# Edges of a graph sorted by half tiles of targets: two scaled one-hots side by side on TensorE, sums of eight fixed pairs kept in PSUM, empty slots masked

## The chip, the cores and the metric

The kernel runs on one core of a Trainium2 chip. The core has TensorE (PE), VectorE (DVE), ScalarE (ACT), GpSimd (POOL) and SyncE (SP), each with its own queue of instructions, and 16 DMA engines that all queues share. The metric is the device time of one execution in microseconds (us).

## What is computed

A layer over 3125 nodes of 512 features and 50000 edges. A node's features are a scalar part of 128 and three vector parts of 128. The layer is a graph convolution plus linear attention, followed by a mixture of eight experts of which each node takes two. The change is in the graph convolution, whose edge part is this:

```python
w = ssp(edge_attr @ W_f1) @ W_f2 * (ssp(s0 @ W_s1) @ W_s2)
w1, w2, w3, w4 = jnp.split(w, 4, axis=-1)
x0e, x1e = split_irreps(x[edge_src])
sh0, sh1 = (edge_sh[:, 0], edge_sh[:, 1:4])
out0 = w1 * x0e * sh0[:, None] + w4 * (jnp.einsum('eum,em->eu', x1e, sh1) / jnp.sqrt(3.0))
out1 = w2[:, :, None] * x0e[:, :, None] * sh1[:, None, :] + w3[:, :, None] * x1e * sh0[:, None, None]
edge_feat = merge_irreps(out0, out1)
out = jax.ops.segment_sum(edge_feat, edge_dst, num_segments=old_x.shape[0])
```

Each edge has four numbers sh. Each of the eight products of weights and source features is multiplied with one of them, and the results are summed over the edges of a target node. The part s0 needs, for each edge, the products of the vector parts at its two ends.

## The kernel before

**Tiles of edges.** Edges come in any order. The kernel sorts them by tiles of 125 targets (TG, 25 tiles), so that the sum over edges becomes a product of a one-hot matrix (edge to target in the tile) with the features. Edges are taken 128 at a time; two such blocks are a pair (PR = 2), two pairs a quad (G = 4 blocks). A tile gets as many pairs as its edges need; 204 pairs are always run (NPR_MOST), and 16 more stand in a branch for data that needs them.

**The sort and the node work (lines 129 to 654).** DVE counts the edges of each tile (line 201, one instruction for each of 25 tiles), and `places` (lines 230 to 252) ranks the edges of a chunk of 28 blocks: a comparison of tiles (235), a running sum (239), a product (243), a reduction (244), and some index arithmetic. `records` builds a record of 48 numbers for each edge (sh, source, target, place in the tile, hidden activations) and writes it to memory in line. Then POOL scatters the records to their sorted places, 391 indirect DMAs of 128 records (417). `place` lets POOL go on only as far as PE has come in the node work beside it. All slots of the sorted list are zeroed first (166, 10 DMAs from POOL), since a tile's last pair has empty slots.

**The edge loop (lines 709 to 978).** Order on PE, ACT, DVE and POOL is written out by hand in `run_pairs`. One step s handles, of different pairs: `fetch` (four indirect gathers on POOL, two of 1664 and two of 3584 bytes a row; nine pairs ahead), `products` (DVE, both ends of an edge), `turn` and `hidden` (PE: transposes and small products, for a quad), `softplus` (ACT), `weigh` (PE makes two factors of the weights, ACT scales the first and copies it, DVE multiplies), `dots` and `dots2` (ACT and DVE: the sum over sh of the vector parts), `feats` (DVE, and six ACT scalings by sh: 1024 features for each edge), `which` (DVE: the one-hot, 128 wide), `gather_up` and `keep_sums`:

```python
for k in range(PR):
    for m in range(2):
        nc.tensor.matmul(
            R.ps, R.one[:, k, :], R.ft[:, k, m * D : (m + 1) * D],
            start=(k == 0 and m == 0), stop=(k == 1 and m == 1),
        )
```

Four matrix products of 512 columns give a pair's sums in PSUM; each appears in the profile as two instructions (passes)[...]. DVE then adds them to the tile's row of acc. `line_up` copies the experts' weights into another layout, memory to memory, 32 DMAs of 1 MB on POOL's queue, one in every sixth step.

**The experts (from line 983).** Tile by tile, own rows are loaded (1020), the sums of acc are transformed and added, stored (1031), normed and stored again (1051). Then the gates, index arithmetic and 53 expert tiles.

Of the kernel before, what the change touches and what calls it, by code (L numbers as in the profile page):

```python
# [16 lines left out]
P = 128  # L17
EDGES = 50000
TG = 125
D = 512  # L20
# [11 lines left out]
NPR_MOST = 204  # L32
# [13 lines left out]
def gnn_mix_moe_kernel(ctx: ExitStack, tc: tile.TileContext, a: dict, out: bass.AP):  # L46
# [13 lines left out]
    NPR = (EDGES - NG) // (PR * P) + NG  # L60
    whole, rest_e = divmod(EDGES, P)
    TE = whole + (rest_e > 0)
    NQ = (NPR * PR + G - 1) // G
# [29 lines left out]
    pair_tile = const.tile([P, NPR], I32, name="pair_tile")  # L93
# [4 lines left out]
    lined = dram.tile([T // CT, P, CT, REC], F32, name="lined")  # L98
    recs = dram.tile([NQ * G * P, REC], F32, name="recs")

# [19 lines left out]
    tok = counted(const, "tok", [[TG, NT]], [P, NT], channel=1)  # L120
# [8 lines left out]
    with ExitStack() as c1:  # L129
        srt = c1.enter_context(tc.tile_pool(name="srt", bufs=1))  # L130
        ints = c1.enter_context(tc.tile_pool(name="ints1", bufs=1))
        pair_no = counted(srt, "pair_no", [[1, NPR]], [P, NPR])
# [21 lines left out]
        for r in range(4):  # L154
# [5 lines left out]

        zw = NQ * G * REC // 10
        zero = tmp.tile([P, zw], F32, name="zero")
        nc.vector.memset(zero, 0.0)
        flat = recs.rearrange("s f -> (s f)")
        cleared = [
            nc.gpsimd.dma_start(
                flat[k * P * zw : (k + 1) * P * zw].rearrange("(p f) -> p f", p=P), zero
            )
            for k in range(10)
# [16 lines left out]
        in_tile_i = tmp.tile([P, T], I32, name="in_tile_i")  # L186
        nc.vector.tensor_scalar(in_tile_i, to_i, 4195.0, None, op0=ALU.mult)
        nc.vector.tensor_single_scalar(in_tile_i, in_tile_i, 19, op=ALU.arith_shift_right)
        in_tile = tmp.tile([P, T], F32, name="in_tile")
        nc.vector.tensor_copy(in_tile, in_tile_i)  # L190
        to_f = tmp.tile([P, T], F32, name="to_f")
        nc.vector.tensor_copy(to_f, to_i)
        local = tmp.tile([P, T], F32, name="local")
        nc.vector.scalar_tensor_tensor(local, in_tile, -float(TG), to_f, op0=ALU.mult, op1=ALU.add)

        NC = T // CT
        hot = tmp.tile([P, NT, CT + 1], F32, name="hot")
        sums = tmp.tile([P, NT], F32, name="sums")
        here = tmp.tile([P, T], F32, name="here")
        for b in range(NT):  # L200
            nc.vector.tensor_scalar(
                here, in_tile, float(b), 0.0, op0=ALU.is_equal, op1=ALU.add, accum_out=sums[:, b : b + 1]
            )
        ps_c = psum.tile([P, NT], F32, name="ps_c", tag="mm")
# [224 lines left out]
        for c in range(1, NC):  # L429
            records(c)  # L430
            for t in range((c - 1) * NT // (NC - 1), c * NT // (NC - 1)):
                place(8 * t + 42)
                place(8 * t + 50, layer_norm(t))
# [997 lines left out]
```

## Time and profile before

| what | value |
|---|---|
| median of 3 runs | 2956.8 us (2954.85 to 2974.9) |
| the profiled execution | 2957.7 us, its span 2955.8 us |
| PE busy | 2533.0 us, 86% |
| DVE busy | 1785.0 us, 60% |
| POOL busy | 1719.6 us, 58% |
| ACT busy | 1393.6 us, 47% |
| first scatter of records | 79.23 us |
| first gather of the edge loop | 721.87 us |
| first aggregation (line 902) | 774.41 us |
| last addition to acc (line 911) | ends 2022.8 us |

The page has the busy time of each engine, the same in 40 slices of the span, and groups of instructions by line. In a group's row come line, engine, operation, output and inputs, shapes and count; then its busy time and the mean ns of one; then the time for which its engine stood idle before it, and what ended that. A row of the timeline has start, duration, engine, line, operation, and in brackets the idle time before it. PEld is the loading of PE's stationary operand.

### The profile page before, as it was taken

What the parts mean: (1) busy time and instruction counts of PE and PEld (TensorE: products, weight loads), DVE (VectorE), ACT (ScalarE), POOL (GpSimd) and SP (SyncE); (2) the same over time, 40 slices, a digit from 0 to 9 for tenths busy, and PEclk for the clock granted to TensorE, in tenths of its full rate; (3) what the DMA queues carried; (4) which work ended last, traced back from release to release, by engine and by line L of the source; (5) the groups of instructions that cost most, each with busy time, mean ns of one, the idle gap of its engine ahead of it and who ended that gap; (6) DMA issues with size and microseconds to landing.
All of it is one profiled execution on the core that took longest, in us unless ns stands there. A gap on an engine that the chain in (4) does not pass through costs nothing. (4 is left out here: it accounts for less than half of the span.)

```text
span 2955.8 us, 44464 instructions
## 1 busy us (share of the span) xinstructions
PE 2533.0 (86%) x14742; PEld 1593.7 (54%) x14742; DVE 1785.0 (60%) x3666; ACT 1393.6 (47%) x3960; POOL 1719.6 (58%) x1723
## 2 busy tenths in 40 slices
PE   2466594885699999999999999997599999999997
PEld 2344242553344444444444444445488888888886
DVE  4755450223699999999999999998422222222221
ACT  1334241110588888877888888885211111111111
POOL 0766657664766666666666666641355555555552
PEclk9767796897799999999999999999799999999998
DMA  6435202554788888787888888855722623956361
GB/s 259 148 126 175 85 21 66 168 174 137 245 256 255 256 255 254 256 248 247 254 259 262 261 263 262 253 177 187 279 66 72 239 69 119 329 202 244 112 223 51
DMA packets 189190, 577.23 MB, mean 195 GB/s; under 512 B 54177, under 2 KB 78662, under 8 KB 176920
## 3 DMA queue, kind: packets, MB, share of 16 engines
q0 software_dynamic: 132912, 485.72, 51.1%
q1 hardware_dynamic: 49704, 82.29, 8.2%
q10 hardware_dynamic: 6336, 6.28, 0.7%
q8 instruction: 121, 1.98, 0.3%
q14 instruction: 117, 0.96, 0.1%
HBM read 624.55 MB, written 119.50 MB: 252 GB/s over the span
## 5 line engine op out<-in xcount | busy, mean ns | idle before, releaser
L902 PE MATMUL ps_s<-ft,one 128*128 128x512 f32 x1632 | 745.7, 600 | 19.4 <-issue 14.2
L730 POOL DMA_INDIRECT gd<-rows_d,rec x408 | 434.4, 1065 | 269.0 <-issue 87.2
L417 POOL DMA_INDIRECT recs<-again,at_i x391 | 400.8, 1025 | 231.6 <-issue 110.5
L902 PEld LDWEIGHTS ps_s<-ft,one 128*128 128x128 f32 x1632 | 294.1, 190 | 396.0 <-issue 318.7
L734 POOL DMA_INDIRECT gx<-rows_s,rec x408 | 400.9, 983 | 144.8 <-issue 102.4
L885 ACT ACTIVATE ft<-ft,rec 128x128 f32<-128x128 f32 x1224 | 380.2, 389 | 201.9 <-DVE ft L878 143.0
L1306 ACT ACTIVATE h<-ps_f,bias 128x128 f32<-128x128 f32 x318 | 110.7, 367 | 671.5 <-PE ps_f L1293 622.1
L1293 PE MATMUL ps_f<-h,we 128*128 128x128 f32 x3392 | 406.8, 278 | 16.7 <-ACT h L1306 15.1
L1293 PEld LDWEIGHTS ps_f<-h,we 128*128 128x128 f32 x3392 | 388.8, 192 | 30.7 <-ACT h L1306 25.0
L1308 DVE TENSOR_SCALAR h<-ps_f,bias 128x128 f32<-128x128 f32 x318 | 108.2, 350 | 481.6 <-PE ps_f L1293 456.9
L1220 POOL DMA_INDIRECT we<-w_rows,w_at x212 | 214.3, 1011 | 266.6 <-PE ps_y L1324 102.0
L830 DVE TENSOR_TENSOR wt<-wt,wb 128x1024 f32<-128x1024 f32 x204 | 247.6, 1214 | 29.9 <-PE ps_h L775 21.9
L840 ACT ACTIVATE dot<-gx,rec 128x128 f32<-128x128 f32 x816 | 261.4, 398 | 0.0
L819 PE MATMUL wa<-w_f,hT 32*128 32x512 f32 x816 | 240.2, 642 | 3.7 <-issue 2.6
L823 PE MATMUL wb<-w_s,hT 32*128 32x512 f32 x816 | 241.7, 644 | 0.0
L1293 PEld LDWEIGHTS ps_f<-xt,we 128*128 128x128 f32 x1696 | 200.1, 194 | 26.0 <-issue 24.9
L746 DVE TENSOR_TENSOR prod<-gd,gx 128x768 f32<-128x768 f32 x204 | 194.0, 951 | 31.0 <-DMA gx<-rows_s,rec 31.0
L1293 PE MATMUL ps_f<-xt,we 128*128 128x128 f32 x1696 | 200.5, 277 | 0.7 <-ACT xt L1241 0.7
L754 PEld LDWEIGHTS ps_ip<-ident,prod 128*128 128x128 f32 x1224 | 136.3, 144 | 118.7 <-issue 118.7
L889 DVE TENSOR_TENSOR ft<-gx,wt 128x768 f32<-128x768 f32 x204 | 197.6, 969 | 0.0
L1324 PE MATMUL ps_y<-we,h 128*128 128x512 f32 x424 | 196.1, 605 | 0.2
L754 PE MATMUL ps_ip<-ident,prod 128*128 128x128 f32 x1224 | 161.3, 283 | 40.7 <-issue 40.7
(306 smaller groups left out, 3599.2 us busy)
## 6 DMA issues: line engine op xcount, KB each, us to landing
w_rows<-in_Wh POOLq DMA_DIRECT2D x24, 1024.0 KB
rows_s<-r SPq DMA_DIRECT2D x24, 448.0 KB
recs<-zero POOLq DMA_DIRECT2D x10, 1056.0 KB
rec<-recs SPq DMA_DIRECT2D x102, 96.0 KB
lined<-rec SPq DMA_DIRECT2D x14, 672.0 KB
again<-lined POOLq DMA_DIRECT2D x14, 672.0 KB
w_rows<-in_Wo POOLq DMA_DIRECT2D x8, 1024.0 KB
gd<-rows_d,rec POOLq DMA_INDIRECT x408
```

The costliest lines, as they stand in the source:

```text
L417: put = nc.gpsimd.indirect_dma_start(out=recs[:, :], out_offset=bass.IndirectOffsetOnAxis(ap=at_i[:m, t : t + 1], axis=0), in_=again[c][:m ...
L730: nc.gpsimd.indirect_dma_start(out=Q.gd[:, (i + 2) % G, :], out_offset=None, in_=rows_d[:, :], in_offset=bass.IndirectOffsetOnAxis(ap=reci ...
L734: Q.last = nc.gpsimd.indirect_dma_start(out=Q.gx[:, i, :], out_offset=None, in_=rows_s[:, :], in_offset=bass.IndirectOffsetOnAxis(ap=reci[ ...
L754: nc.tensor.matmul(ps[:, i, :], Q.prod[:, i, b * P : (b + 1) * P], ident, is_transpose=True, start=(b == 0), stop=(b == 2),)
L819: nc.tensor.matmul(wa[:, k, :], Q.hT[r, 0, :], w_f2[r, :], start=True, stop=True)
L823: nc.tensor.matmul(wb[:, k, :], Q.hT[r, 1, :], w_s2[r, :], start=True, stop=True)
L830: nc.vector.tensor_mul(R.wt, R.wt, wb)
L840: nc.scalar.activation(R.dot[:, c - 1, k, :], x[:, i, c * MUL : (c + 1) * MUL], AF.Copy, scale=Q.rec[:, i, c : c + 1])
L885: nc.scalar.activation(R.ft[:, k, D + c * MUL : D + (c + 1) * MUL], R.ft[:, k, 2 * D :], AF.Copy, scale=Q.rec[:, i, c : c + 1],)
L902: nc.tensor.matmul(R.ps, R.one[:, k, :], R.ft[:, k, m * D : (m + 1) * D], start=(k == 0 and m == 0), stop=(k == 1 and m == 1),)
L1220: nc.gpsimd.indirect_dma_start(out=dst, out_offset=None, in_=src, in_offset=bass.IndirectOffsetOnAxis(ap=at[:, j : j + 1], axis=0), bounds ...
L1293: nc.tensor.matmul(pss[f], ws[l][:, k, f * P : (f + 1) * P], h[:, k, :], start=(k == 0), stop=(k == 3))
```

## The change

It does six things.

- Edges are sorted by half tiles: the first 63 and the last 62 targets of a tile's 125. The first block of each pair holds edges of the first half, the second block those of the second. A tile always has eight pairs (PER), so room for 1024 edges a half; what is over goes to 12 overflow pairs at the end (NOV_MOST), and to a loop behind a branch if that isn't enough. 200 + 12 pairs are always run.
- A slot that holds no edge isn't zeroed in memory any more (only each tile's last quad and the overflow pairs are); its record is masked on DVE when it is loaded (`clear`).
- The one-hot is 64 wide, made once for a quad, and ACT makes four copies of it, scaled by the four sh (`scaled`). The features are then no longer scaled: `dots` and `dots2` go, with six scalings on ACT and a multiplication on DVE, and all six products of vector parts come from two DVE multiplications.
- The aggregation has four products a block, one of 512 and three of 256 columns; the two blocks of a pair use the columns 0 to 63 and 64 to 127 of the array.
- The sums of a tile's eight pairs stay in PSUM, and ACT copies them to acc once; only overflow pairs are added on DVE.
- The copies of the experts' weights go to ACT's queue and are written beside the sort and the node work. In the experts' part a tile has 128 rows, so loads and stores come in half tiles, and index arithmetic maps rows to nodes.

```diff
-        in_tile_i = tmp.tile([P, T], I32, name="in_tile_i")
-        nc.vector.tensor_scalar(in_tile_i, to_i, 4195.0, None, op0=ALU.mult)
+        in_half_i = tmp.tile([P, T], I32, name="in_half_i")
+        nc.vector.tensor_scalar(in_half_i, to_i, 4194.0, 1500.0, op0=ALU.mult, op1=ALU.add)
...
-        for b in range(NT):
+        for b in range(NU):
             nc.vector.tensor_scalar(
-                here, in_tile, float(b), 0.0, op0=ALU.is_equal, op1=ALU.add, accum_out=sums[:, b : b + 1]
+                here, in_half, float(b), 0.0, op0=ALU.is_equal, op1=ALU.add, accum_out=sums[:, b : b + 1]
...
             nc.vector.tensor_tensor(
-                hot[:, :, 1:], in_tile[:, c * CT : (c + 1) * CT].unsqueeze(1).to_broadcast([P, NT, CT]),
-                lane[:, :NT].unsqueeze(2).to_broadcast([P, NT, CT]), op=ALU.is_equal,
+                hot[:, :, 1:], in_half[:, ts].unsqueeze(1).to_broadcast([P, NU, CT]),
+                lane[:, :NU].unsqueeze(2).to_broadcast([P, NU, CT]), op=ALU.is_equal,
             )
...
+        def line_up(behind):
+            if not mats:
+                return
+            e, l = mats.pop(0)
+            src = a["Wh"][e, l] if l < NL else a["Wo"][e]
+            with tc.issue_after(behind.ins):
+                nc.scalar.dma_start(
+                    w_rows[l][e * P : (e + 1) * P, :].rearrange("p (k f) -> p k f", k=4),
+                    src.rearrange("(k p) f -> p k f", p=P),
+                )
...
-                place(8 * t + 50, layer_norm(t))
+                normed = layer_norm(t)
+                place(8 * t + 50, normed)
+                line_up(normed)
...
                 place(275 + 5 * (2 * c + g), last)
+                line_up(last)
...
+        def clear(Q, real):
+            reci = Q.rec.bitcast(I32)[:, :, :USED]
+            nc.vector.tensor_tensor(
+                reci, reci, real.rearrange("p s k -> p (s k)").unsqueeze(2).to_broadcast([P, G, USED]),
+                op=ALU.bitwise_and,
+            )
...
+        def which(Q):
+            Q.one = work.tile([P, G, HT], F32, name="one")
+            nc.vector.tensor_tensor(
+                Q.one, lane[:, :HT].unsqueeze(1).to_broadcast([P, G, HT]),
+                Q.rec[:, :, 6:7].to_broadcast([P, G, HT]), op=ALU.is_equal,
+            )
...
+        def scaled(R):
+            R.ones = work.tile([P, PR, 4, HT], F32, name="ones", bufs=3)
+            for k, i in enumerate(R.tiles):
+                for c in range(4):
+                    nc.scalar.activation(
+                        R.ones[:, k, c, :], R.Q.one[:, i, :], AF.Copy, scale=R.Q.rec[:, i, c : c + 1]
+                    )
...
             R.wt = work.tile([P, PR, D], F32, name="wt")
-            for k, i in enumerate(tiles):
-                nc.scalar.activation(
-                    R.wt[:, k, : 2 * MUL], wa[:, k, : 2 * MUL], AF.Copy, scale=Q.rec[:, i, 0:1]
-                )
-            nc.scalar.copy(R.wt[:, :, 2 * MUL :], wa[:, :, 2 * MUL :])
+            nc.scalar.copy(R.wt, wa)
             nc.vector.tensor_mul(R.wt, R.wt, wb)
...
             nc.vector.tensor_mul(
-                ends,
-                R.wt.rearrange("p k (b c u) -> p k b c u", b=2, c=2)[:, :, :, 0, :],
-                x[:, :, :MUL].unsqueeze(2).to_broadcast([P, PR, 2, MUL]),
-            )
...
+                ends, w[:, :, :, 0, :], x[:, :, :MUL].unsqueeze(2).to_broadcast([P, PR, 2, MUL]),
+            )
+            for k in range(PR):
+                nc.vector.tensor_mul(
+                    R.ft[:, k, MUL : 7 * MUL].rearrange("p (b c u) -> p b c u", b=2, c=3),
+                    w[:, k, :, 1, :].unsqueeze(2).to_broadcast([P, 2, 3, MUL]),
+                    x[:, k, MUL:].rearrange("p (c u) -> p c u", c=3).unsqueeze(1).to_broadcast([P, 2, 3, MUL]),
+                )
+
+        def gather_up(R, ps, first, last):
+            for m in range(4):
+                for k in range(PR):
+                    rows = slice(k * HT, (k + 1) * HT)
...
+                    nc.tensor.matmul(
+                        to, R.ones[:, k, m, :], what, start=(first and m == 0), stop=(last and m == 3),
+                        tile_position=(0, k * HT),
                     )
...
+            def kept(at):
...
+                if at >= NFIX:
+                    keep_sums(tile_of(pair_tile[0:1, at - NFIX : at - NFIX + 1]), R.ps)
+                elif at % PER == PER - 1:
+                    nc.scalar.copy(acc[:, at // PER, :], R.ps)
...
+            for s in range(-LEAD - 5, n_pairs + 1):
+                for Q in due(s + LEAD + 5):
+                    q = quads.index(Q)
+                    loaded = load(Q, recs[q * G * P : (q + 1) * G * P, :])
...
+                for Q in due(s + LEAD + 1):
+                    q = quads.index(Q)
+                    clear(Q, real_slot[:, PR * q : PR * (q + 1), :])
+                for R in pair(s + LEAD):
+                    fetch(R.Q, R.j)
+                for Q in due(s + 2):
+                    softplus2(Q)
+                for Q in due(s + 3):
+                    which(Q)
+                for k in range(2):
+                    for Q in due(s + 7 - k):
+                        products(Q, k)
+                for R in pair(s + 1):
+                    weigh(R)
+                kept(s - 1)
...
-                    nc.gpsimd.dma_start(out[rows, :], base[:n, t, :])
+                    for k in range(2):
+                        i0 = t * TG + k * (HT - 1)
+                        m = HT - 1 - k
+                        nc.gpsimd.dma_start(out[i0 : i0 + m, :], base[k * HT : k * HT + m, t, :])
```

## The prediction

> **What bounds the kernel now.** I read first the busy slices of the page, then a table of busy time by stretch. It gives four stages: sorting and node work (0 to 717 us), filling the edge pipeline (717 to 774), the edge loop (774 to 2023), and the gated experts. In the table each engine has its busy time and, in brackets, its instructions; then come the clock granted to PE, the share of the DMA engines and GB/s.
>
> ```profile
> core 0: us, PE busy (x) PEld busy (x) DVE busy (x) ACT busy (x) POOL busy (x), PEclk, DMA share, GB/s
> 79.00:360.00 281.00, 164.83 (x586) 108.29 (x586) 158.20 (x500) 105.68 (x217) 203.06 (x193) 0.76 0.43 139
> 774.00:1960.00 1186.00, 1159.83 (x6568) 540.56 (x6564) 1141.88 (x2025) 968.45 (x2990) 814.30 (x805) 1.00 0.81 256
> ```
>
> In the edge loop PE and DVE are both full (98% and 96%), ACT has 82%, POOL looks free at 69%. The aggregation of line 902 ran 1536 times between 780 and 1960 us, eight instructions a pair: 192 pairs, 6.13 us each. The timeline shows one pair on DVE; the first column is the start, so differences of starts are what an instruction really costs:
>
> ```profile
> 1970.53 0.68 DVE L911 TENSOR_TENSOR acc<-acc,ps_s 128x512 f32 x1
> 1971.13 1.22 DVE L830 TENSOR_TENSOR wt<-wt,wb 128x1024 f32<-128x1024 f32 x1
> 1972.38 0.69 DVE L878 TENSOR_TENSOR ft<-wt,gx 128x512 f32<-128x512 f32 x1
> 1972.99 0.95 DVE L889 TENSOR_TENSOR ft<-gx,wt 128x768 f32<-128x768 f32 x1
> 1973.86 0.42 DVE L894 TENSOR_TENSOR ft<-wt,dot 128x256 f32<-128x256 f32 x1
> 1974.19 0.41 DVE L860 TENSOR_TENSOR one<-lane,rec 128x256 f32<-128x256 f32 x1
> 1974.53 0.42 DVE L848 TENSOR_TENSOR dot<-dot 128x256 f32<-128x256 f32 x1
> 1974.98 0.62 DVE L850 SCALAR_TENSOR_TENSOR dot<-gx,rec,dot 128x128 f32<-128x128 f32 x2
> 1975.51 0.95 DVE L746 TENSOR_TENSOR prod<-gd,gx 128x768 f32<-128x768 f32 x1
> ```
>
> No gap stands between them: 5.85 us, and 6.05 in every other pair, which has line 801 as well. So **DVE sets 5.95 us** of the 6.13.
>
> POOL is not as free as it looks. The groups of the loop, then the timeline of the filling, where POOL waits for nobody:
>
> ```profile
> L730 POOL DMA_INDIRECT gd<-rows_d,rec x349 | 371.4, 1064 | 213.4 <-issue 73.2 <-DVE one L860 46.3 <-PE ps_h L775 39.8
> L734 POOL DMA_INDIRECT gx<-rows_s,rec x348 | 341.1, 980 | 123.0 <-issue 87.2 <-ACT ft L885 32.8 <-ACT wt L829 1.8
> ...
> 733.21 0.94 POOL L734 DMA_INDIRECT gx<-rows_s,rec  x1 [0.30 <-issue]
> 734.46 0.95 POOL L730 DMA_INDIRECT gd<-rows_d,rec  x1 [0.30 <-issue]
> 735.55 0.96 DVE L746 TENSOR_TENSOR prod<-gd,gx 128x768 f32<-128x768 f32 x1 [3.86 <-DMA gx<-rows_s,rec]
> 735.72 1.61 POOL L734 DMA_INDIRECT gx<-rows_s,rec  x1 [0.30 <-issue]
> ```
>
> A gather takes 0.95 us and 0.30 stand before the next, so the four of a pair need at least 5.0 us. The one at 735.72 began while DVE multiplied two SBUF tiles, and took 0.66 more: it got going when DVE was done. With only that product beside it POOL needed 5.5 us a pair here (products at 735.55, 741.11, 746.59). In the loop the stretch averages 0.07 us a gather, so POOL could do 5.3.
>
> **What the Trainium skill says.** "SBUF — State Buffer", section "Who interferes with whom": a DVE tensor_tensor with both inputs in SBUF contends with a GpSimd instruction that reads SBUF, and the second to start waits for the first to end. The trace agrees (the 0.66 us); multiplications with one input in PSUM (line 830) stretched no gather. "TensorEngine Tiling (Array Packing)", section "Tiling Modes": tiles in different columns load and multiply in parallel, but a change of mode drains the array. The trace agrees on the first, at 32 columns:
>
> ```profile
> 1308.56 0.43 PE L770 MATMUL ps_h<-ident,rec 128*32 128x128 f32 x8
> 1308.80 0.40 PE L775 MATMUL ps_h<-ident,gd 128*32 128x128 f32 x8
> 1309.02 0.40 PE L780 MATMUL ps_h<-ip,w_s1c 128*32 128x128 f32 x8
> ```
>
> These 24 passes of 128 columns end after 0.86 us. A pass of 512 columns costs 0.43 us in line 902 (0.19 of loading and 0.24 of idle), so one of 128 costs 0.107, and 24 in a row 2.57. No run shows 64 columns. "Trainium Kernel Development and Optimization", section "Key Constraints": DMAs from the SP, ACT and POOL queues run on the same 16 engines.
>
> **The change, part by part.** Its sum is made against the profiled execution, 2957.7 us (span 2955.8), 0.9 above the median of 2956.8.
>
> DVE, per pair. Gone: the sum over acc 0.60, line 894 0.33, lines 848 and 850 0.98, half of the one-hot 0.17 (256 wide once in two pairs, not in each). New: a second multiplication of 768 elements, 0.87, and the mask of 160 elements in each quad, between the 0.20 of 128 and the 0.33 of 256, halved to 0.12. 5.95 - 2.08 + 0.99 = **4.86 us**.
>
> PE, per pair. The aggregation took 3.60 to 3.70 us for 8 passes of 512 columns; now 4 of 512 and 12 of 256, or 5120 columns for 4096. One after the other that is 4.56 us; two at a time 2.28, and one pass of offset makes 2.7. A quad took 11.35 us (aggregations at 1300.33 and 1311.68), so 5.7 a pair; less 1.0, plus some 0.2 for changes of mode: **4.9 us**.
>
> ACT, per pair. It was 968.45 / 1186 of 6.13, or 5.0. Gone: ten scalings at 0.31 (1.86 for six), and 0.5 as three copies of 0.83 + 0.57 become one of some 0.9. New: eight scalings half as wide, 0.27 each by the slope of line 829 against line 826. About 3.6 us; it hides.
>
> POOL, per pair. Four gathers as before, 5.0, and the stretches. DVE now has three multiplications of 0.87, one of 0.61 and half of mask and one-hot that hold the port. If gathers start at any time in them, the mean wait is the sum of half squares, (3 x 0.82^2 + 0.56^2 + 0.06) / 2 / 5.5 = 0.22, with each hold cut by the 0.13 us by which the stretches stay under the remainder: 5.9 us a pair. The loop's own 0.07 gives 5.3, the filling's case 5.5. I take **5.55**, so POOL becomes the bound. Behind it DVE's products wait for rows, which land 3.8 us after the fourth gather (737.33 to 741.11). The DMA engines were at 0.79 in 740 to 760 us with POOL unhindered, so they do not bind.
>
> The loop then has 212 pairs, not 204 (200 fixed and 12 for overflow; with this data 10 overflow pairs are needed, so the late branch stays untaken, as the branch of before did at 203). 212 x 5.55 = 1177, 4 for the landing, nine pairs without gathers at 4.9 = 44: 1225 us. Before it was 721.9 to 2022.8, 1301. Gain: **76 us**.
>
> The sorting. Counting 50 half tiles, not 25, adds 25 x 0.65 us on DVE before the first edge is placed at 79 us, and the first chunk's ranks 4.5: +20. Zeroing falls from 10.8 MB to 3 MB, which may free the 11 us that DVE waited for sh at 45 us: -5. Then 13 chunks of ranks with DVE steps twice as wide. POOL scatters here at 1.27 us an edge block; of 198 scatters 18 met the scan of line 239 and stretched by 0.56 each, 10 us. Holds twice as long cost four times that: +30, and +10 for the two compares. POOL idled 34 us at 360 to 394 for PE, which takes most of it in: +10 remain. The 32 weight copies (33.5 MB) leave POOL's queue in the loop and go to ACT's queue here. At the loop's 256 GB/s they are 131 us of DMA time on top of 0.43 x 281 = 121: 90% of this stretch, which it may just hold: +13. Issuing them takes ACT up to 1.4 us each (W_kT at 7.02), hidden by its 62% of idle time, unless they stand ahead of its first activation. Together **+38**; bounds -20 and +120, since the trace does not show such copies beside the sort.
>
> The rest. Clearing acc (10.7 us) ran beside the wait for the records: 0. The expert stage reads and writes two half tiles where it had one: POOL 2 x 0.53 us in a period of 1.31, just hidden; four small DVE steps on the gather indices, 0.8 us; two stores of normed rows become one. **+2**. SP's more loads go ahead of need.
>
> 2957.7 - 76 + 38 + 2 = **2922 us**; as a median, 2921.
>
> **The rivals.**
> First, the forecast: POOL binds at 5.3 to 5.9 us, 2849 (with +20 of sorting) to 3010 (with +60). Chance 0.55.
> Second, the slower side: the first stage pays. The line that is to hold the copies back names a PE instruction, while they are ACT's, and copies that wait for nothing could stand at the head of ACT's queue. There 131 us of traffic share the engines with the first loads of edges, and scatters start at some 180, not 79 us. +100 against the 76 gives about 3005; it decides from a growth of 106 us in the first stage. For it: DMA was at 0.74 in the first 50 us and DVE waited 24.6 and 11.1 us for sh. Against: the queues take turns. Chance 0.22.
> Third, the halves do not run side by side: PE at 5.7 + 0.9 + 0.2 = 6.8 us, 212 x 6.8 = 1442 and 52 of filling, +193 and +40: 3190. The 0.86 us speak against. Chance 0.06.
> Fourth, gathers fall between DVE's holds and the sort stays hidden: 5.05 us, 1119, -182 and +10: 2788. Chance 0.17.
>
> **The numbers.** A difference under 1% (29.6 us) can't be told from none here. Faster: 0.33 of the first and all of the fourth, 0.50. Same: 0.16 of the first and 0.08 of the second, 0.24. Slower: the rest, 0.26. The range of 2800 to 3040 leaves out most of the third and a part of the fourth and of the second; the first alone has 2850 to 3010.
>
> **What would show it.** PE in the loop well under 90% with POOL's gaps at 0.30; the new aggregation at 2.3 to 2.9 us a pair; gathers of 1.05 to 1.15 us mean; DVE waiting at line 746 for rows; first scatter at 90 to 105 us; first gather at 740 to 780. Wrong would be: scatters starting past 150 us, an aggregation over 4 us, or a period over 6 us a pair.

## The result, and the profile after

The changed kernel took 3145.3 us (median of 4 runs, 3138.9 to 3157.3), the kernel before 2955.8 us: a ratio of 1.065, 95% interval 1.058 to 1.071. It is slower, by 190 us; 2921 us were forecast. The profiled execution has a span of 3137.2 us, 181.4 more than the 2955.8 of the kernel before. By stage:

| stage | before | after | difference | forecast |
|---|---|---|---|---|
| start to the first gather | 721.9 | 742.7 | +20.8 | +38 |
| first gather to the last sum | 1300.9 | 1470.8 | +169.9 | -76 |
| experts | 933.0 | 923.7 | -9.3 | +2 |

So the whole loss is in the edge loop. The measurements of this study fell on two kinds of occasions, **short** ones, on which the kernel before took 2770 to 2784 us (but for single runs of 2980 and 7487 us, which are left out), and **long** ones like that of the result, on which it took 2942 to 3036 us, so a kernel is compared only with runs of the kernel before on the same occasion.

The table of busy time for the edge loop after the change:

```profile
core 0: us, PE busy (x) PEld busy (x) DVE busy (x) ACT busy (x) POOL busy (x), PEclk, DMA share, GB/s
797.00:2100.00 1303.00, 1112.00 (x8057) 523.70 (x8049) 937.78 (x1249) 719.59 (x2223) 845.52 (x770) 0.88 0.69 207
```

No engine is full: PE 85%, DVE 72%, POOL 65%. PE's clock, which was 1.00, is 0.88, and the DMA engines moved 207 GB/s where they moved 256. The groups of the loop say who waits:

```profile
L829 POOL DMA_INDIRECT gx<-rows_s,rec x424 | 483.7, 1141 | 262.1 <-DVE ft L949 138.5 <-issue 105.7 <-DVE prod L840 10.9
L825 POOL DMA_INDIRECT gd<-rows_d,rec x424 | 445.7, 1051 | 266.5 <-issue 108.1 <-PE ps_h L866 98.9 <-DVE rec L813 29.2
L931 DVE TENSOR_TENSOR wt<-wt,wb 128x1024 f32<-128x1024 f32 x212 | 258.4, 1219 | 382.4 <-ACT wt L930 236.9 <-remote 95.5 <-ACT ones L913 17.1
L840 DVE TENSOR_TENSOR prod<-gd,gx 128x768 f32<-128x768 f32 x212 | 202.3, 954 | 33.9 <-DMA gx<-rows_s,rec 21.5 <-remote 7.9 <-issue 4.5
```

POOL waits for DVE and PE to release gx and gd; DVE waits for ACT's copy of wa, and ACT for PE. A pair takes 6.70 us on the mean (differences of starts of line 931), but the median is 5.90: half of the pairs take 4.9 to 6, and about one in four 7.9 to 10.9. The timeline of PE in such a pair; "issue" stands where the engine waited for nothing that the profile shows:

```profile
895.66 2.37 PE L969 MATMUL ps_s<-ft,ones 128*64 128x512 f32 x16
...
900.83 0.41 PE L861 MATMUL ps_h<-ident,rec 128*32 128x128 f32 x4 [1.08 <-DVE rec L813]
902.03 0.38 PE L861 MATMUL ps_h<-ident,rec 128*32 128x128 f32 x2 [0.79 <-issue]
902.75 0.27 PE L861 MATMUL ps_h<-ident,rec 128*32 128x128 f32 x1 [0.34 <-issue]
903.46 0.37 PE L861 MATMUL ps_h<-ident,rec 128*32 128x128 f32 x1 [0.43 <-issue]
903.49 0.41 PE L866 MATMUL ps_h<-ident,gd 128*32 128x128 f32 x1
904.20 0.37 PE L866 MATMUL ps_h<-ident,gd 128*32 128x128 f32 x1 [0.30 <-issue]
904.90 0.63 PE L866 MATMUL ps_h<-ident,gd 128*32 128x128 f32 x2 [0.33 <-issue]
906.32 0.46 PE L866 MATMUL ps_h<-ident,gd 128*32 128x128 f32 x2 [0.78 <-issue]
...
907.34 3.73 PE L969 MATMUL ps_s<-ft,ones 128*64 128x512 f32 x16
```

The aggregation at 895.66 takes 2.37 us, within the 2.3 to 2.9 forecast. But from 900.8 to 906.3 PE's small products come at 902.03, 902.75, 903.46, 904.20, 904.90: one step each 0.71 us, though the profile shows nothing that they wait for. The same 16 passes took 0.64 us in the kernel before (1308.56 to 1309.20 in the prediction). The aggregation after them takes 3.73 us, since the clock has fallen. Windows of 3.41 us, the step of the clock's records, show which came first:

```profile
896.60:900.01 3.41, 3.08 (x22) 1.00 (x18) 3.32 (x4) 1.07 (x5) 2.50 (x4) 1.00 0.87 283
900.01:903.42 3.41, 1.06 (x7) 0.47 (x8) 1.64 (x4) 0.64 (x2) 2.80 (x3) 0.98 0.74 222
903.42:906.84 3.42, 1.97 (x15) 1.00 (x16) 0.00 (x0) 2.22 (x9) 1.23 (x2) 0.50 0.85 249
906.84:910.25 3.41, 3.41 (x18) 1.36 (x14) 2.69 (x3) 3.05 (x10) 0.94 (x1) 0.52 0.50 165
```

First PE's instructions thin out (7 products in the second window, at 0.98 of the clock; 0.8 us of its idle time is the wait for DVE's rec); the clock is halved from the next window on. POOL gathers all the while, and its own timeline ends with the stretch:

```profile
902.76 0.95 POOL L825 DMA_INDIRECT gd<-rows_d,rec  x1 [0.30 <-issue]
904.01 0.94 POOL L829 DMA_INDIRECT gx<-rows_s,rec  x1 [0.30 <-issue]
907.26 0.94 POOL L825 DMA_INDIRECT gd<-rows_d,rec  x1 [2.30 <-PE ps_h L866]
912.97 0.95 POOL L829 DMA_INDIRECT gx<-rows_s,rec  x1 [4.77 <-DVE prod L840]
```

POOL's last gather of a series ends at 904.95, and by 906.3 PE runs again. This mostly repeats every 27.4 us, four pairs: 15 or 16 gathers with 0.30 us between them, PE slow from about the twelfth on, everything behind PE late, POOL out of buffers, and PE free again. Counted over the loop from the starts of PE's products and weight loads together: of 144 gaps of 0.69 to 0.73 us, 143 lie in a series of gathers or less than 1 us after it, and each of the 40 series of 14 or more gathers has some. Such series, with the 1 us, cover 82% of the time from 800 to 2150 us, so this count points to POOL but proves little by itself. Below, "slow gaps" are these, counted from 60 us after the first gather to 30 us before the last sum (146 here); "half clock" is the time at half clock in the same stretch (324 us here; 7 us and 14 slow gaps in the kernel before). With products alone there are fewer: the expectation of g2_pace3 says 97.

### The profile page after: what moved, and what is told of

It is laid out like the page before. It is cut to its first block, busy times and chain, and to the rows that moved or that the text cites. A ratio compares the mean times of both kernels' runs of the same rounds, so it can differ in the third digit from the quotient of the medians.

```text
span 3137.2 us, 46186 instructions
## 1 busy us (share of the span) xinstructions
PE 2525.6 (81%) x16716; PEld 1592.3 (51%) x16716; DVE 1684.5 (54%) x3084; ACT 1162.2 (37%) x3261; POOL 1822.3 (58%) x1741
## 5 line engine op out<-in xcount | busy, mean ns | idle before, releaser
L829 POOL DMA_INDIRECT gx<-rows_s,rec x424 | 483.7, 1141 | 262.1 <-DVE ft L949 138.5
L969 PE MATMUL ps_s<-ft,ones 128*64 128x256 f32 (+1 forms) x3392 | 588.2, 481 | 17.8 <-issue 15.2
L825 POOL DMA_INDIRECT gd<-rows_d,rec x424 | 445.7, 1051 | 266.5 <-issue 108.1
L459 POOL DMA_INDIRECT recs<-again,at_i x391 | 425.8, 1089 | 236.0 <-issue 111.6
L913 ACT ACTIVATE ones<-one,rec 128x64 f32<-128x64 f32 x1696 | 428.1, 339 | 0.0
L969 PEld LDWEIGHTS ps_s<-ft,ones 128*64 128x64 f32 x3392 | 254.8, 149 | 301.5 <-issue 238.0
L949 DVE TENSOR_TENSOR ft<-wt,gx 128x768 f32<-128x768 f32 x424 | 386.0, 952 | 0.0
L930 ACT COPY wt<-wa 128x1024 f32<-128x1024 f32 x212 | 214.3, 1011 | 424.6 <-PE wb L928 207.0
L928 PE MATMUL wb<-w_s,hT 32*128 32x512 f32 x848 | 270.8, 655 | 11.2 <-issue 8.3
L924 PE MATMUL wa<-w_f,hT 32*128 32x512 f32 x848 | 252.9, 650 | 7.5 <-issue 5.7
L840 DVE TENSOR_TENSOR prod<-gd,gx 128x768 f32<-128x768 f32 x212 | 202.3, 954 | 33.9 <-DMA gx<-rows_s,rec 21.5
```

What stands on the lines that cost most here:

```text
L459: put = nc.gpsimd.indirect_dma_start(out=recs[:, :], out_offset=bass.IndirectOffsetOnAxis(ap=at_i[:m, t : t + 1], axis=0), in_=again[c][:m ...
L825: nc.gpsimd.indirect_dma_start(out=Q.gd[:, (i + 2) % G, :], out_offset=None, in_=rows_d[:, :], in_offset=bass.IndirectOffsetOnAxis(ap=reci ...
L829: nc.gpsimd.indirect_dma_start(out=Q.gx[:, i, :], out_offset=None, in_=rows_s[:, :], in_offset=bass.IndirectOffsetOnAxis(ap=reci[:, i, 4:5 ...
L913: nc.scalar.activation(R.ones[:, k, c, :], R.Q.one[:, i, :], AF.Copy, scale=R.Q.rec[:, i, c : c + 1])
L924: nc.tensor.matmul(wa[:, k, :], Q.hT[r, 0, :], w_f2[r, :], start=True, stop=True)
L928: nc.tensor.matmul(wb[:, k, :], Q.hT[r, 1, :], w_s2[r, :], start=True, stop=True)
```

## The experiments

Three theories of the half clock stood first: IDLE, LOAD and STALL, as the expectations say. Diffs are against the changed kernel.

**e1_zero**: features of zero.

```diff
+        nc.vector.tensor_single_scalar(w_f2, w_f2, 0.0, op=ALU.mult)
```

> The changed kernel with w_f2 multiplied by zero once before the edge loop, so that wa, wt and the features ft that the aggregation streams are all zero; every instruction stays (the messages are left out of the result). Three theories of the 324 us at half clock in the edge loop. IDLE (PE is no longer the full engine, has windows of little work, and loses its clock for it): nothing changes, 3145 us within 30, half clock for 280 to 370 us of the loop. LOAD (two column halves at once draw too much, and the clock is taken for that): zeros draw less, half clock under 80 us, time 2880 to 2950. STALL (something else holds PE's instructions back every 27 us and the clock only follows): as IDLE.

**e2_serial**: the halves one after the other.

```diff
-            for m in range(4):
-                for k in range(PR):
+            for k in range(PR):
+                for m in range(4):
```

> The changed kernel with the two loops of gather_up exchanged: all passes of one half, then all of the other, so that halves no longer run side by side. Same result. The aggregation goes from 2.37 to some 4.4 us a pair and PE is full at 6.8 to 7.1 us a pair. IDLE: a full PE keeps its clock, half clock under 60 us of the loop, 212 x 6.9 = 1463 us of loop and 3110 to 3190 us in all, the same as the changed kernel although 2 us of PE work a pair came on top. LOAD: the clock stays too, same time. STALL: half clock stays over 200 us, time over 3300 us.

**e3_warm**: wa made twice.

```diff
                 nc.tensor.matmul(wa[:, k, :], Q.hT[r, 0, :], w_f2[r, :], start=True, stop=True)
+            for k, i in enumerate(R.tiles):
+                r = slice(i * HID, (i + 1) * HID)
+                nc.tensor.matmul(wa[:, k, :], Q.hT[r, 0, :], w_f2[r, :], start=True, stop=True)
```

> The changed kernel with the products for wa (line 924) made twice, the second time over the first: 4 more passes of 512 columns on PE in each pair, some 0.6 us, same result. IDLE: PE has fewer windows with little work, half clock falls from 324 to under 150 us of the loop, and the time falls, to 2960 to 3080 us, though work was added. LOAD and STALL: half clock stays at 300 us or more, time 3200 to 3280 us.

**e4_light**: half of the aggregation.

```diff
-            for m in range(4):
+            for m in (0, 3):
```

> The changed kernel with half of the aggregation left out (the sums over the first two vector components, m = 1 and 2): 1.1 us less PE work a pair, everything else as it was. IDLE: more windows with little work, half clock at 324 us or more of the loop, and the time hardly falls: 3050 to 3150 us. LOAD: less is drawn, half clock under 150 us, time 2850 to 2930 us. STALL: half clock at 250 to 330 us, time 3000 to 3100 us.

All four missed on the time, since this was a short occasion: 2769.1, 2821.5, 2766.3 and 2766.3 us, where the kernel before took 2777.5. That called for both kernels as they are.

> The changed kernel itself, once more, beside the four edits of the first experiments, which took 2766 to 2821 us where the kernel before took 2777.5 and not 2955.8. SUPPLY (in the first profiles PE's instructions came for stretches one each 0.71 us although nothing held them, in the kernel before as well, and the changed kernel, which hands PE 84 instructions a pair in place of 68 and in bursts, pays more for it; the edits did nothing of weight): 2755 to 2785 us here, half clock in the edge loop under 150 us, hardly a gap of 0.69 to 0.73 us between PE's instructions. LOAD or IDLE (the edits did it, each in its own way): 3100 us or more here, with 0.71 us gaps and 280 us or more at half clock.

> The kernel before itself, for its profile at 2777 us. SUPPLY: its first stage is shorter by 60 to 100 us (first gather at 620 to 660 us, not 722), its edge loop by 50 to 70 (5.85 to 5.95 us a pair as DVE's own instructions set it, not 6.13), its experts by 30 to 40, and the 40 gaps of 0.69 to 0.73 us between PE's instructions are gone. Otherwise the 180 us come from one stage alone.

The changed kernel took 2768.0 us and the kernel before 2777.4, a ratio of 0.997 (0.996 to 0.998). No slow gaps worth the name are left (2 and 0). The kernel before has its first gather at 613.0 us, a loop of 1257.7 (5.95 us a pair) and 898.4 us of experts; the changed kernel 649.5, 1228.4 (5.59 us a pair) and 891.2. SUPPLY named the place rightly, if not each size: the long occasion costs the kernel before 109 us of the first stage, 43 of the loop and 35 of the experts. The groups of the changed kernel on the short occasion:

```profile
L829 POOL DMA_INDIRECT gx<-rows_s,rec x424 | 504.1, 1189 | 134.0 <-issue 115.5 <-DMA gx<-rows_s,rec 5.3 <-DMA gd<-rows_d,rec 4.3
L825 POOL DMA_INDIRECT gd<-rows_d,rec x424 | 417.1, 984 | 133.9 <-issue 107.0 <-DVE wt L931 18.0 <-DMA rec<-recs 4.5
L840 DVE TENSOR_TENSOR prod<-gd,gx 128x768 f32<-128x768 f32 x212 | 203.4, 959 | 161.9 <-DMA gx<-rows_s,rec 161.4
L861 PE MATMUL ps_h<-ident,rec 128*32 128x128 f32 x848 | 47.7, 299 | 147.8 <-DVE hT L891 147.8
```

This is the loop that was forecast: POOL's idle time is the bare 0.30 us a gather, a gather takes 1.09 us, and DVE waits for rows at line 840.

With that, the four edits can be read as to the clock. PE is full in e2_serial (half clock 0 us), nearly so in e3_warm (7), less in the changed kernel (99, and 99 with zeros) and least in e4_light (253). So the clock follows PE's idle time, and not the data: LOAD falls. The table of busy time for a0_after and for e4_light, in this order, has the clock last but two:

```profile
700.00:1820.00 1120.00, 973.65 (x8376) 490.99 (x8376) 979.42 (x1297) 750.37 (x2325) 871.52 (x802) 0.96 0.83 250
```

```profile
700.00:1820.00 1120.00, 917.16 (x6776) 410.73 (x6774) 977.66 (x1297) 738.11 (x2320) 873.25 (x801) 0.89 0.84 249
```

The loops of the two take 1228.4 and 1228.6 us. So half clock alone costs nothing here. IDLE explains the clock and not the time.

**e5_psh2 and e6_lined** asked what sets the loop on a short occasion.

```diff
+        both_h = ps_a.tile([P, 2, 2, P], F32, name="both_h")
...
-            Q.ps = ps_a.tile([P, 2, P], F32, name="ps_h")
+            Q.ps = both_h[:, (quads.index(Q) if Q in quads else 0) % 2]
```

> The changed kernel with two buffers for ps_h in one bank, in turns by quad, so that PE need not wait in hidden for hT of the quad before (86.6 us of PE's waiting in the first profile). If that wait is on the path of the loop: 20 to 60 us less than the changed kernel on the same chip. If POOL's gathers set the period: within 8 us of it.

```diff
-            with tc.issue_after(behind.ins):
-                nc.scalar.dma_start(
+            nc.gpsimd.dma_start(
...
+                if s >= 0 and s % 6 == 0:
+                    line_up(None)
```

> The changed kernel with the 32 weight copies back where they were, on POOL's queue in the edge loop, one in six pairs. If POOL's gathers set the loop: the loop grows by 32 issues of about 1 us and by what 33.5 MB more take from the gathers, 30 to 130 us; the first stage falls by 10 to 40 us; together 10 to 100 us slower than the changed kernel on the same chip. If something else than POOL and DMA sets the loop: within 10 us, or faster by the first stage.

e5_psh2 took 2768.2 us, as the changed kernel: PE's wait for hT is not on the path. e6_lined took 2818.1, 50 more; its profiled loop is 38 us longer, and its first gather comes at 652.3 us, not earlier than the 649.5 with the copies in the first stage. So on a short occasion the copies cost the first stage nothing, and POOL's loop 38 us. **e7_ten** shortens the loop by two pairs, and **e8_hold** takes PE away by hand:

```diff
-NOV_MOST = 12
+NOV_MOST = 10
```

> The changed kernel with NOV_MOST at 10 in place of 12, so 210 pairs and not 212 (the overflow needs 10 here; more would go the way of the late branch). If POOL's gathers set the period of the loop: 2 x 5.55 = 11 us less than the changed kernel, 2757 us where the kernel before takes 2777. If PE sets it, as in the first profile, 2 x 6.7 = 13 us less than 3145. No change if the last pairs lie beside something else.

```diff
-            Q.ps = ps_a.tile([P, 2, P], F32, name="ps_h")
+            Q.ps = ps_a.tile([P, 4, P], F32, name="ps_h")
+            if Q in quads and quads.index(Q) % 2 == 0:
+                for i in range(19):
+                    nc.tensor.matmul(Q.ps[:, 2:4, :], ident, w_f2[:, : 2 * P], start=True, stop=True)
```

> The changed kernel with a hold of PE of 8.2 us once in four pairs: 19 products of 256 columns into an unused part of ps_h, ahead of hidden in every second quad. In the first profile of the changed kernel PE lost about that much every 27.4 us: some 5 us in which its instructions came one each 0.71 us, and 3.4 us by 6.8 us at half clock. HOLD ENOUGH (the loss on PE alone makes the longer loop; four pairs of PE work at 4.86 us and 8 us make 27.4): on a chip where the kernel before takes 2777 us, a loop of 27 to 28 us for four pairs, 1430 to 1490 us from the first gather to the last sum, 2960 to 3030 us in all. HOLD COVERED (PE's slack of 0.7 us a pair and the leads of the hand-written order take most of it in): under 2880 us. Where the kernel before takes 2956 us, 300 us and more on top of 3145.

e7_ten took 2760.0 us where the kernel before took 2776.7 (0.994, 0.992 to 0.997), 8 less than the changed kernel for 11 expected. e8_hold took 3041.3 us, its loop 1498.8: 270 more than 1228.4, or 5.1 of the 8.4 us that each hold takes in the trace (8.2 were planned). So four pairs have 3.3 us of cover for PE, and a loss of some 8 us on PE in four pairs is by itself enough for a loop as long as that of the result. HOLD ENOUGH stands, a little above its range. POOL then waits for hidden to release gd, as in the result:

```profile
L825 POOL DMA_INDIRECT gd<-rows_d,rec x424 | 429.2, 1012 | 331.2 <-PE ps_h L869 213.1 <-issue 102.2 <-DVE wt L934 9.4
```

What slows PE down? **e9_both** joins e3_warm and e7_ten; **e10_flat** has fewer PE instructions:

> The changed kernel with NOV_MOST at 10 and with the products for wa made twice (the edits of e7_ten and e3_warm together), the second to keep PE from windows of little work. Where the kernel before takes 2777 us: 2750 to 2765 us, below both kernels, since POOL sets the period and PE has room. Where the kernel before takes 2956 us, as in the first profile: if PE's 0.71 us stretches answer to PE's idle time (IDLE for both), they and the half clock go and the time is 2900 to 2960; if they come whatever PE does (SUPPLY), 3130 us or more.

```diff
+            Q.flat = work.tile([P, 2, P], F32, name="flat", bufs=1)
+            flat = Q.flat.rearrange("p k (i f) -> p k i f", i=G)
+            nc.scalar.copy(flat[:, 0], Q.rec[:, :, 8:USED])
+            nc.scalar.copy(flat[:, 1], Q.gd[:, :, :HID])
...
-            for i in range(G):
-                nc.tensor.matmul(
-                    Q.ps[i * HID : (i + 1) * HID, 0, :], Q.rec[:, i, 8:USED], ident,
...
+            nc.tensor.matmul(Q.ps[:, 0, :], Q.flat[:, 0, :], ident, start=True, stop=True)
+            nc.tensor.matmul(Q.ps[:, 1, :], Q.flat[:, 1, :], ident, start=True, stop=False)
```

> The changed kernel with 72 PE instructions a pair in place of 84: ACT copies the 32 columns of rec and of gd of four tiles side by side (two copies of 128 elements a quad), and hidden turns them with one product of 128 columns each in place of four of 32 (rec2 has 7 buffers and not 8, for room). Same result. Where the kernel before takes about 2960 us: if what is short there is PE's instruction supply (SUPPLY, 12.5 instructions a us over the edge loop of the changed kernel), 12 of 84 less take the loop from 1471 to some 1260 to 1330 us and the time from 3145 to 2930 to 3010 us; if the 0.71 us stretches come at their own times, or answer to PE's idle time, 3100 us or more. Where the kernel before takes 2777 us: POOL sets the period and the time stays at 2755 to 2775 us.

e9_both met a long occasion: 3188.7 us where the kernel before took 2962.7, with 125 slow gaps, although PE had more to do. So it is not PE's idle time that calls them up. e10_flat met a short one (2770.9 beside 2777.3), so it was made again, beside e2_serial:

> The kernel of e10_flat once more (72 PE instructions a pair in place of 84), for a measurement in which the kernel before takes about 2960 us. There SUPPLY expects 2930 to 3010 us, stretches that come at their own times or with PE's idle time expect 3100 us or more. Where the kernel before takes 2777 us it tells nothing new: 2771 us.

> The kernel of e2_serial once more (halves one after the other, 84 instructions a pair, 2 us more PE work a pair), for a measurement in which the kernel before takes about 2960 us. There SUPPLY expects the added work to cost next to nothing, as it runs while instructions are short: 3110 to 3200 us. If PE lost 8 us in four pairs whatever it does, these come on top of a full PE: 212 x (6.2 + 2.0) = 1738 us of loop and 3400 us in all. Where the kernel before takes 2777 us it tells nothing new: 2821 us.

This occasion was long (the kernel before took 2969.2). f1_flat took 3166.6 us, with 127 slow gaps: with 72 instructions or 84 the loss is no smaller (loops of 1505.5 and 1470.8 us, 1232.5 and 1228.4 on short occasions), and SUPPLY as a shortage by number falls. f2_serial took 3175.5 with 49 slow gaps, though each of its pairs has 1.3 us more PE work (an aggregation of 3.7 us, not 2.4): its ratio to the kernel before is 1.071 (1.061 to 1.081), that of the changed kernel 1.065. A set loss of time on PE falls too: 8 us in four pairs, on a PE that is full, would make e2_serial's loop of 1284.6 us 53 x 8 longer, 1709, and f2_serial has 1497.7. In all four long traces, with that of the result, the loop takes 1471 to 1505 us, and of the slow gaps from 800 to 2150 us 114 of 121 (e9_both), 117 of 124 (f1_flat) and 45 of 48 (f2_serial) lie in a series of gathers or less than 1 us after it, where these again cover about 80% of the time. The next edits break the series by a rest on POOL (like e10_flat and f1_flat, they leave rec2 seven buffers, not eight; f1_flat has its 127 slow gaps with seven):

```diff
+        rest = gat.tile([P, 184], I32, name="rest", bufs=1)
...
             if k == 0:
...
+                for _ in range(5):
+                    nc.gpsimd.iota(rest, pattern=[[1, 184]], base=0, channel_multiplier=0)
```

> The changed kernel with a rest on POOL ahead of every eighth gather: five counts into an unused tile, some 1.2 us without a gather in each quad (rec2 has 7 buffers, for room). In the slow profiles of the changed kernel POOL gathers 15 or 16 times without a break, PE's instructions begin to come one each 0.71 us at about the thirteenth, and within 1 us of POOL's stop they flow again; the kernel before breaks off after 8 or 9. Where the kernel before takes about 2960 us: if unbroken gathering is what holds PE up (GATHERS), hardly one 0.71 us gap is left in the loop, four pairs take 24 to 25 us, and the time is 2990 to 3060 us, below 3145 though POOL was given work; if PE's stretches have another cause, the rests come on top or are hidden by POOL's waits: 3130 to 3290 us. Where the kernel before takes 2777 us: POOL sets the period, so 106 x 1.2 = 127 us on 2768, 2860 to 2910.

g1_pace met a short occasion: 2993.4 us beside 2774.6, 225 more than the changed kernel, since the pause with the rest came to 2.2 us a quad, 1.9 more than the 0.30 without, and not 1.2 more. It says only that POOL sets the period there. With three counts, with one (and NOV_MOST at 10), and with two ahead of each pair:

> As g1_pace with three counts and not five: a rest of some 1.5 us between two gathers in each quad, where 0.3 us stood. Where the kernel before takes about 2960 us: if unbroken gathering is what holds PE up (GATHERS), under 25 gaps of 0.69 to 0.73 us between PE's instructions are left in the edge loop (97 in the first profile of the changed kernel), and the time is 2990 to 3050 us, below 3145 although POOL was given work; if PE's stretches have another cause, the gaps stay and the time is 3130 to 3290 us. Where the kernel before takes 2777 us: POOL sets the period, 106 x 1.2 = 127 us on 2768, 2880 to 2910 us.

> As g2_pace3 with one count a quad (some 0.55 us of rest in place of 1.2) and with NOV_MOST at 10. Where the kernel before takes about 2960 us: if so short a rest is enough to keep PE's instructions flowing (GATHERS, any break does), the loop is 105 x 11.7 us and 50, 1280, and the time 2930 to 2970 us, level with the kernel before or below it; if a break must last longer, PE's stretches come back, with over 60 gaps of 0.69 to 0.73 us in the loop, and the time is 3050 to 3150 us. Where the kernel before takes 2777 us: POOL sets the period, 2760 and 105 x 0.55, 2805 to 2830 us.

> The changed kernel with two counts on POOL ahead of each pair's first gather: nearly the rest of g2_pace3 in a quad (2 x 0.55 us for 1.2), in two breaks of half the length (the one count of g3_pace1 came to 0.18 us only, as it began where POOL would have waited 0.30 anyhow). Where the kernel before takes 2950 to 3020 us: if the mean rate of the gathers decides, this does as g2_pace3 did: under 30 gaps of 0.69 to 0.73 us in the loop and 3000 to 3060 us; if a break must have a certain length, they stay over 80, and the time is 3110 to 3200 us. Where the kernel before takes 2777 us: POOL sets the period, 2768 and 106 x 1.1, 2870 to 2900 us.

All three met long occasions.

| run | eight gathers take | slow gaps | loop, us | time | kernel before |
|---|---|---|---|---|---|
| changed kernel | 10.8 | 146 | 1470.8 | 3145.3 | 2955.8 |
| f1_flat | 10.8 | 127 | 1505.5 | 3166.6 | 2969.2 |
| f2_serial | 10.8 | 49 | 1497.7 | 3175.5 | 2969.2 |
| e9_both | 11.0 | 125 | 1505.1 | 3188.7 | 2962.7 |
| g3_pace1 | 11.2 | 125 | 1448.4 | 3128.0 | 3018.6 |
| kernel before | 12.05 | 14 | 1300.9 | 2955.8 | |
| g2_pace3 | 12.4 | 17 | 1355.0 | 3020.8 | 2959.1 |
| g4_spread | 12.9 | 8 | 1413.7 | 3076.2 | 2959.4 |

The second column is the distance from a gather of gd to the fourth after it: the median, and for the five with many slow gaps the tenth percentile, since POOL itself is stopped in the rest of them. The tenth percentiles of the last three are 11.8, 11.9 and 12.4, so the order does not hang on this choice. f2_serial shows that the number of slow gaps does not measure the loss, and that the pace is not all that sets their number.

The loop can also be reckoned for a POOL that is never held up: half the pace for each pair, and the 48 us of the forecast (4 and 44) for the ends. The short occasion bears this out (106 x 11.1 + 48 = 1225 us, measured 1228.4). On the long ones it gives 1362 for g2_pace3 and 1415 for g4_spread, within 7 us of the measured loops, but 1193 for the changed kernel and 1224 for g3_pace1 (105 x 11.2), which took 278 and 224 us more.

g2_pace3 gave POOL more to do and is 124 us faster than the changed kernel: 1.021 of the kernel before (1.010 to 1.032), not 1.065. POOL's timeline in it, with the rest:

```profile
1210.28 1.23 POOL L833 DMA_INDIRECT gx<-rows_s,rec  x1 [0.30 <-issue]
1211.51 1.01 POOL L826 IOTA rest<- 128x184 int32 x3
1213.02 1.68 POOL L829 DMA_INDIRECT gd<-rows_d,rec  x1 [0.50 <-issue]
```

GATHERS hit with the time and the gaps of g2_pace3. In g3_pace1 the second expectation came, slow gaps and 3050 to 3150 us: the single count came to 0.18 us, as it began where POOL would have waited 0.30 anyhow, and freed nothing. g4_spread divides its rest in two breaks of half the length and has the fewest slow gaps, so on a long occasion it is the pace and not the length of a break that decides. Its time missed the range by 16 us, because the four counts cost POOL 1.8 us a quad (12.9 against 11.1), not 1.1.

## Why the prediction was wrong

**The step that failed** is in the part on POOL: "I take 5.55, so POOL becomes the bound", from which 212 x 5.55 and the loop of 1225 us follow, with PE at 4.9 us taken for covered: what gathers at that pace do to PE stood at nothing. As a sum for a POOL that is never held up it was right: on the short occasion a pair took 5.59 us and the loop 1228.4. On the occasion of the result it took 6.70, because a POOL that gathers at 11 us for eight gathers holds PE's instructions up there. What PE loses is some 8 us in four pairs, an estimate: the loop is 242 us longer than on the short occasion, 4.6 us in each four pairs, and the cover of 3.3 us that e8_hold shows is lost first. The forecast gave PE 0.65 us of slack a pair. It let one engine be full and the rest be free, and knew the contention of POOL with DVE only. That POOL set the period did no harm in g2_pace3 and g4_spread; the faster pace of its gathers was the cost.

**The trace of before had a sign of it.** The forecast gave DVE 5.95 of the 6.13 us and left 0.18 unexplained. The median pair took 5.98 us; 17 of 195 took 6.6 to 9.4, and 9 of these 17 have a slow gap on PE. The timeline of DVE in one of them, in the kernel before:

```profile
947.46 0.68 DVE L911 TENSOR_TENSOR acc<-acc,ps_s 128x512 f32 x1
950.02 1.22 DVE L830 TENSOR_TENSOR wt<-wt,wb 128x1024 f32<-128x1024 f32 x1 [1.88 <-PE ps_h L775]
```

DVE waits 1.88 us for PE there, and PE's own row at that time has an idle time that the page puts down to "issue":

```profile
949.92 0.38 PE L780 MATMUL ps_h<-ip,w_s1c 128*32 128x128 f32 x2 [0.56 <-issue]
```

The averages of 98% and 96% hid these pairs. On the short occasion, which has none of them, the loop of before is 1258 us, so the gain down to 1225 is only 33 us, less than the 38 given to the sort: even with PE never held up the sum comes to no change. That is what the short occasion measured: +36.5 for the first stage, -29.3 for the loop, -7.2 for the experts, and a ratio of 0.997.

**Point by point.** The aggregation was forecast at 2.3 to 2.9 us, measured 2.37; gathers at 1.05 to 1.15, measured 1.10; the first scatter at 90 to 105, measured 90.6; the first gather at 740 to 780, measured 742.7. PE in the loop was well under 90%, as forecast (85%), but POOL's gaps were not at 0.30 us: it stood idle for 529 us ahead of the gathers, and only 214 of these were the bare 0.30. "Wrong would be ... a period over 6 us a pair" is what came. DVE's wait for rows came on the short occasion only (161.9 us, against 33.9). The sort's +38 was met on the short occasion (+36.5) and was +20.8 on the long one, but its 13 us for the copies was not: e6_lined shows no cost of theirs there. The contention of DVE and POOL that the Trainium skill states ("SBUF — State Buffer", "Who interferes with whom") set POOL's 5.59 us as reckoned, and the trace agrees: on the short occasion the 403 gathers that began beside the DVE products of lines 840 and 949, with both inputs in SBUF, took 0.29 us longer on the mean, and the 48 beside line 931, with one input in PSUM, took none longer.

**The rivals.** The first (POOL binds) was right in mechanism on short occasions and wrong for the result. The second (+100 in the first stage) did not come: scatters started at 90.6 us. Its sum was off as well, since 2957.7 + 100 - 76 and the 2 of the rest make 2984 and not 3005, unless some 20 us of the sort's own are added. The third named a time near the result, 3190 us, for a reason that is not so: the halves run side by side, 2.37 us against 3.71 in e2_serial, and even e2_serial's loop took 1284.6 us, not 1494 (1442 and 52 of filling), since 5120 columns in a row cost 3.71 us and not the 4.56 reckoned. That f2_serial's 1497.7 us lie near it is chance. None of the four had a POOL that slows PE down.

**The half clock** looked like the cause and is not. "TensorE: Matmul & The Clock Gate", section "Part 1: The HAM clock gate", of the Trainium skill says that PE's clock halves after an idle window of about 3.4 us. The trace agrees with the step of 3.41 us, but a window in which PE worked for 1.06 us of its 3.41 was followed by a halved clock as well. It adds to a stretch that has another cause: g2_pace3 has 229 us of half clock and 17 slow gaps, e4_light 253 us and no loss.

**What stays open.** Why PE's instructions thin out on some occasions and not on others is not known: the short occasion has the same pace of 11.1 us and 2 slow gaps. The chips numbered 6 and 8 had one of each, so the number of the chip does not tell. It is not the landing of rows: from the packets in the trace, a gather of gx has landed 3.24 us after its instruction on the long occasion and 3.22 on the short. Nor is it a late packet of PE's instructions: one comes about every 20 us, and the last one before a stretch stands at no fixed distance, 0.2 to 21 us ahead. That POOL's pace decides on a long occasion is shown by g2_pace3, g3_pace1 and g4_spread; by what path it reaches PE is not shown. A slower POOL also starts fewer transfers at a time, and no run separates POOL's instructions from the transfers that they start. The mean of the bytes moved does not decide: the kernel before moved 256 GB/s over its loop on a long occasion and had 14 slow gaps. On a long occasion no version beat the kernel before (g2_pace3 came nearest). On a short one e7_ten beats both.

## What to carry to other kernels

Before an engine is made the bound, ask what it does to others when it never rests: here, on long occasions, POOL at 11 us for eight gathers cost PE an estimated 8 us in four pairs, and a rest of 1.2 us won back 124 us of the time. Read the spread of a loop's period and not only its mean; a few long turns with a wait for "issue" in them can be the sign of a second limit that a change brings forward. And when the kernel before itself takes two times on different occasions, only pairs of the same occasion can be compared.

## What the runs showed of the hardware

PE's instructions can come one each 0.71 us for some 5 us with no wait that the profile shows, while POOL gathers fast: 0 and 2 slow gaps in the loops of the two kernels on short occasions, on long ones 49 to 146 at 10.8 to 11.2 us for eight gathers and 8 to 17 at 12.05 to 12.9. Halves of 64 columns side by side do 16 passes (4 of 512 columns, 12 of 256) in 2.37 us, one after the other in 3.71, a factor of 1.57 and not 2. A half clock for 253 us of the loop cost nothing in e4_light, where POOL set the period (1228.6 us of loop against 1228.4 with 99 us of half clock).
